# Attention and feed-forward block: kept instruction order in the front, one norm scaling, and the down projection by seven block products

## The chip, the cores and the metric

The kernel runs on one core of one Trainium2 chip. The metric is the device time of one execution in microseconds (us). Times shown are those of three runs; beside them one execution was taken by the hardware profiler. TensorE (PE) multiplies matrices, VectorE (DVE) and ScalarE (ACT) work elementwise, GpSimd (POOL) works elementwise too, and SyncE (SP) issues most transfers.

## The reference, cut to what matters

All values are fp32. There are 8 batches of 128 tokens with 512 features.

```python
n  = layernorm(x)                              # over the features, no weights
r  = n * rsqrt(mean(n*n) + 1e-5) * ln_weight   # a second norm of the same rows
q, k, v = r @ Wq.T, ctx @ Wk.T, ctx @ Wv.T     # 32 heads of 128
p  = softmax(q k^T + bias, masked)             # no scaling by the head size
x1 = x + n + (p v) @ Wo.T
m  = layernorm(x1)
h  = silu((m @ Wg.T) * ag) * ((m @ Wu.T) * au) # 1376 wide
y  = x1 + (h @ Wd.T) * ad
```

## The kernel before, in words

All tokens (1024) are worked on together. The heads come in eight groups of four. Large products are not taken directly: each operand is cut into 2 x 2 blocks, and the product is put together from seven block products instead of eight. Their operands are sums and differences of blocks, called S1, S2, S4 (made by `sums_a`, L215 to L221, of the weights) and T1, T2, T4 (made by `sums_b`, L223 to L229, of the tokens), and one difference that overwrites a block on each side (L219, L227). `seven` (L248) goes through the products in the order 2, 1, 6, 7, 4, 5, 3; ScalarE copies some results out of PSUM (L259, L269), VectorE adds the others to them (L264, L275). Products 6, 7 and 4 go into the banks of product 1, so each waits until the result before it was read.

The stages, in order:

- *Front.* The keys and values of group 0 are made from the context (`kv`, L396), as soon as the weights and the context land. Between their products, `norm1` (L183) makes both norms of each batch of x: moments on VectorE, a square root on ScalarE and a reciprocal on VectorE, y = (x - mean) * rstd on VectorE, a square with accumulation on ScalarE, a second root and reciprocal, and a second scaling on ScalarE. `norm1_T` (L202) transposes the result on PE and writes it into hT with the norm's weight. `combine_tokens` (L239) makes the token sums of the context (ctx_sb) and then of hT. GpSimd makes the weight sums S_k, S_v and S_q.
- *Queries* of all eight groups, written to DRAM (L437 to L446).
- *Attention*, group by group, with the keys and values of the next group between the heads' products.
- *Output projection* with the seven products, the residual (`residual`, L580) and the second norm.
- *Feed-forward.* Eleven slices of 128 of the inner width, the last 96 wide. Slices 2i and 2i+1 are one round of the loop at L724: `seven` again, with gate and up side by side. GpSimd makes the sums S_g and S_u of the weights of the coming round. `gated` (L687) then takes a sigmoid on ScalarE and two multiplications on VectorE; the gatings of a round are called during the next.
- *Down projection* (L762). For each batch, eleven matmuls over the slices collect in one bank (the last batch in two halves). VectorE multiplies by ad (L774) and adds the residual x1 (L775), and SyncE stores the rows (L776).

In what order each engine takes its instructions is set by a scheduler from the program, its costs and its dependencies; program order is one input to it. Where an engine is wrapped in `InOrder` (L37), each call is marked to stay in program order relative to the other marked calls of that engine:

```python
def call(*args, **kw):
    return self.tc.keep_in_program_order(getattr(self.engine, op)(*args, **kw))
```

Before the change only TensorE is wrapped so, and only for the last group of the attention. Tiles with one tag share a fixed number of buffers; a tile waits until the buffer it takes over is free.

Of the kernel before, what the change touches and what calls it, by code (L numbers as in the profile page):

```python
# [10 lines left out]
F32 = mybir.dt.float32  # L11
# [38 lines left out]
def xattn_ffn_kernel(  # L50
# [97 lines left out]

    lnw_sb = const.tile([P, DC], F32, name="lnw_sb")
# [81 lines left out]
    def combine_rows(name, w):  # L231
# [5 lines left out]
        return sums_a(nc.gpsimd, a11, a12, a21, a22, s1, s2, s4)  # L237

    def combine_tokens(src):  # L239
# [6 lines left out]
        return sums_b(nc.vector, b11, b12, b21, b22, t1, t2, t4, nc.gpsimd)  # L246

    def seven(name, tiles, product, part, pool, tag="mm"):  # L248
# [13 lines left out]
        for t in tiles:  # L262
            product(1, t, m[t], True)
            nc.vector.tensor_tensor(part(1, 1, t), part(1, 1, t), m[t], ADD)  # L264
            yield
# [6 lines left out]
        for i, r, c in ((5, 2, 2), (3, 1, 2)):  # L272
            for t in tiles:
                product(i, t, m[t], i == 5)
                nc.vector.tensor_tensor(part(r, c, t), part(r, c, t), m[t], ADD)  # L275
                yield
# [119 lines left out]
    def kv(g, out):  # L396
# [3 lines left out]
        keys = project_T(f"k{g}", combine_rows(f"k{g}", wk), ctx_t, kT)  # L400
# [258 lines left out]
    actp = pool("act", NI, reuse_waits="tile")  # L659
# [160 lines left out]
```

## Time and profile before

| what | value |
|---|---|
| median of 3 runs | 1146.57 us (1145.29 to 1150.09) |
| profiled execution | 1144.65 us |
| its span, first to last instruction | 1142.9 us |
| mean granted TensorE clock | 0.994 |
| first query matmul starts | 68.25 us |
| first down-projection matmul starts | 1063.34 us |
| last store is issued | 1140.1 us |

The profile gives each engine's busy time, the instructions in order of time with what ended the idle time before each, and the chain of work that ended last. Line numbers are those of the kernel before. "PEld" is the loading of weights into TensorE, which overlaps its matmuls. An fp32 matmul leaves two records on PE.

### The profile page before, as it was taken

The page shows a single profiled execution, that of the slowest core. Times are in us where ns is not written, and L with a number is a line of the kernel's source. Part 1 is how long each engine was busy: PE and PEld are TensorE (multiplying, and loading weights), DVE is VectorE, ACT ScalarE, POOL GpSimd, SP SyncE. Part 2 cuts the span into 40 slices and gives each one's busy share as a digit, 9 for nine tenths or more (in the row PEclk, how much of TensorE's full clock was granted, in tenths as well). Part 3 has the DMA queues.
Part 4 walks back from the last instruction along what each step waited for, and adds up shares of the span by engine and source line. Part 5 has one row for each costly group of instructions (what it writes and reads, how often), then busy time and mean ns, then how long its engine had stood idle before and what let it go on. Part 6 is the DMA issues. An engine that isn't in the chain of part 4 may idle for free.

```text
span 1142.9 us, 12312 instructions
## 1 busy us (share of the span) xinstructions
PE 1116.1 (98%) x4286; PEld 729.4 (64%) x4286; DVE 505.2 (44%) x957; ACT 317.5 (28%) x899; POOL 298.4 (26%) x255
## 2 busy tenths in 40 slices
PE   7899999999999999999999999889999999999998
PEld 3564444445867778685868679778888864444445
DVE  4541111116555565555555767653434342434311
ACT  2511112223343444443443443221000022233000
POOL 5531221116333333332311633510000314220000
PEclk9999999999999999999999999989999999999999
DMA  9114433257646555565555466765232602110000
GB/s 281 47 37 146 177 119 111 110 183 263 181 133 208 157 184 167 175 194 168 178 166 165 144 193 217 228 198 159 90 104 63 227 8 74 37 37 1 18 28 28
DMA packets 117533, 154.38 MB, mean 135 GB/s; under 512 B 12032, under 2 KB 71680, under 8 KB 117472
## 3 DMA queue, kind: packets, MB, share of 16 engines
q1 hardware_dynamic: 114784, 149.93, 41.0%
q10 hardware_dynamic: 2192, 2.10, 0.6%
q0 software_dynamic: 496, 1.58, 0.5%
q8 instruction: 34, 0.56, 0.2%
q14 instruction: 27, 0.22, 0.1%
HBM read 101.14 MB, written 52.43 MB: 134 GB/s over the span
## 4 chain that ended last, share of the span: by engine, by line
PE 90%; DVE 4%; DMA 3%; ACT 1%; issue 1%; POOL 0%; SPq 0%; ACTq 0%; DVEq 0%; POOLq 0%
PE mm_q L285 17%; PE mm_v L303 16%; PE mm_k L285 14%; PE m L500 13%; PE mm_f L739 9%; PE dn L770 7%; PE sc L325 4%; PE m L45 4%; PE av L381 4%; DMA a<-att 1%; DMA wv<-in_wvT_dram 1%; ACT s L335 1%; PE av L45 1%; PE tp L176 1%; PE gp L704 1%
## 5 line engine op out<-in xcount | busy, mean ns | idle before, releaser
L320 POOL TENSOR_TENSOR s<-pb,mneg 128x512 f32<-128x512 f32 x64 | 81.6, 1275 | 278.9 <-DVE tt L358 238.6
L285 PE MATMUL mm_k<-ctx_sb,wk 128*128 128x512 f32 x256 | 119.4, 610 | 8.8 <-DMA wk<-in_wkT_dram 4.7
L303 PE MATMUL mm_v<-wv,ctx_sb 128*128 128x256 f32 x512 | 115.9, 379 | 0.5 <-DMA wv<-in_wvT_dram 0.5
L285 PE MATMUL mm_q<-hT,wq 128*128 128x512 f32 x256 | 112.5, 592 | 0.0
L335 ACT ACTIVATE s<-s,nmx 128x128 f32<-128x128 f32 x256 | 99.5, 390 | 34.5 <-DVE nmx L332 34.5
L303 PEld LDWEIGHTS mm_v<-wv,ctx_sb 128*128 128x128 f32 x512 | 95.3, 190 | 14.5 <-DMA wv<-in_wvT_dram 1.3
L386 ACT COPY aT<-av 128x512 f32<-128x512 f32 x64 | 37.5, 585 | 210.9 <-issue 125.4
L285 PE MATMUL mm_k<-ctx_sb,S_k 128*128 128x512 f32 x192 | 87.2, 598 | 3.6 <-POOL S_k L218 2.6
L285 PEld LDWEIGHTS mm_q<-hT,wq 128*128 128x128 f32 x256 | 48.6, 190 | 60.8 <-issue 60.7
L285 PEld LDWEIGHTS mm_k<-ctx_sb,wk 128*128 128x128 f32 x256 | 47.6, 195 | 62.5 <-issue 42.1
L303 PE MATMUL mm_v<-S_v,ctx_sb 128*128 128x256 f32 x384 | 86.7, 381 | 0.0
L285 PE MATMUL mm_q<-hT,S_q 128*128 128x512 f32 x192 | 85.0, 592 | 0.0
L328 DVE TENSOR_TENSOR s<-sc,s 128x512 f32<-128x512 f32 x64 | 44.1, 689 | 85.6 <-PE sc L325 73.8
L303 PEld LDWEIGHTS mm_v<-S_v,ctx_sb 128*128 128x128 f32 x384 | 71.6, 190 | 10.5 <-DVE v L275 1.5
L770 PE MATMUL dn<-wd,act 128*128 128x512 f32 (+3 forms) x198 | 75.8, 545 | 0.0
L275 DVE TENSOR_TENSOR q<-q,mm_q 128x512 f32<-128x512 f32 x32 | 22.0, 687 | 114.9 <-PE mm_q L285 114.9
L500 PE MATMUL m<-wo,a 128*128 128x256 f32 x300 | 72.6, 379 | 0.0
L325 PEld LDWEIGHTS sc<-k,q 128*128 128x128 f32 x448 | 58.7, 192 | 14.8 <-issue 13.4
L285 PEld LDWEIGHTS mm_q<-hT,S_q 128*128 128x128 f32 x192 | 36.5, 190 | 45.9 <-issue 45.9
L285 PEld LDWEIGHTS mm_k<-ctx_sb,S_k 128*128 128x128 f32 x192 | 35.0, 190 | 47.6 <-issue 35.4
L770 PEld LDWEIGHTS dn<-wd,act 128*128 128x128 f32 (+1 forms) x198 | 37.6, 190 | 38.5 <-issue 37.4
L500 PEld LDWEIGHTS m<-wo,a 128*128 128x128 f32 x300 | 56.5, 190 | 7.4
(168 smaller groups left out, 1609.5 us busy)
## 6 DMA issues: line engine op xcount, KB each, us to landing
queries<-q SPq DMA_DIRECT2D x32, 512.0 KB, 3.7
q<-queries SPq DMA_DIRECT2D x32, 512.0 KB, 4.4
turned<-tt SPq DMA_DIRECT2D x64, 256.0 KB, 2.2
pT<-turned SPq DMA_DIRECT2D x256, 64.0 KB, 2.4
att<-aT SPq DMA_DIRECT2D x64, 256.0 KB, 2.3
a<-att SPq DMA_DIRECT2D x32, 512.0 KB, 3.4
wq<-in_wqT_dram SPq DMA_DIRECT2D x8, 1024.0 KB, 5.4
wk<-in_wkT_dram SPq DMA_DIRECT2D x7, 1024.0 KB, 5.8
```

The lines of the kernel that those rows point to most:

```text
L45: return self.tc.keep_in_program_order(getattr(self.engine, op)(*args, **kw))
L285: nc.tensor.matmul(out, w[i][:, c, bass.ts(t, P)], src[i][:, c, :], start=(first and c == 0), stop=(c == HC - 1), skip_group_check=True,)
L303: nc.tensor.matmul(out[:, bass.ts(k, HW)], src[i][:, c, bass.ts(2 * t + k, S)], w[i][:, c, :], start=(first and k == 0 and c == 0), stop=( ...
L320: nc.gpsimd.tensor_tensor(s, pb, mneg[:, b : b + 1, :].to_broadcast([P, GH, S]), ALU.add)
L325: tensor.matmul(sc[:, j, :], qT[:, j, bass.ts(b % 2, S)], kT[j][:, cols], start=True, stop=True)
L328: nc.vector.tensor_tensor(s, sc, s, ALU.add)
L335: nc.scalar.activation(s[:, j, :], s[:, j, :], AF.Exp, bias=nmx[:, j : j + 1], accum_out=sm[:, j : j + 1],)
L381: tensor.matmul(av[:, j, :], v[b // 2][:, b % 2, bass.ts(j, P)], pT[:, :, j, :], start=True, stop=True,)
L386: nc.scalar.copy(aT, av)
L500: tensor.matmul(m[n], sa[n][:, c, :], wo_t[g][n][:, c, :], start=(g == order[0] and c == 0 and k % 2 == 0), stop=(g == order[-1] and c == ...
L739: nc.tensor.matmul(out, ws[t][n][:, c, :], h2_t[n][:, c, :], start=(first and c == 0), stop=(c == HC - 1), skip_group_check=True,)
L770: nc.tensor.matmul(o, act[ic][:m, bass.ts(b, S)], wd[:m, ic, cols], start=(n == 0), stop=(n == NI - 1),)
```

## The change

Four things change.

- *Order.* VectorE and GpSimd are wrapped in `InOrder` from the start up to the queries. The context's sums are called one by one between the key products (`ctx_sums`), the four sums of each weight stay together, and the moments, the scaling and the transposes of a batch are placed at written positions. The wrapped work includes the sums of hT.
- *One norm scaling.* Both norms become one scaling by 1/sqrt(v (1 + eps) + eps^2), with v the variance: no y, no square, no second root; ScalarE scales and shifts x directly. The first norm's own rstd, which the residual needs, is made for all batches at once.
- *Down projection by seven products.* The inner slices in pairs (even, odd), the batches b and b + 4, and the two halves of the output columns are the blocks. `weigh_down` multiplies wd by ad on GpSimd and makes its differences there, one step at each `seven` product of rounds 1 to 3, in kept order. `a_sums` makes the sums of the gated values on VectorE. For each pair of batches `down` takes seven products over five pairs of slices and four matmuls for the last slice; `down_out` adds the results into x1 on ScalarE, VectorE and GpSimd, and x1 is stored.
- *Tiles.* The gated values lie in three tiles instead of eleven, and the sigmoid's tile comes from the work pool.

```diff
@@ -146,6 +146,9 @@
         nc.sync.dma_start(x_in[b // 2][:, b % 2, :], x[b])
     q_w = {0: load_q(0)}
+    vector, gpsimd = InOrder(tc, nc.vector), InOrder(tc, nc.gpsimd)
...
@@ -180,28 +183,30 @@
     mv1 = const.tile([P, B, 2], F32, name="mv1")
     rs1 = const.tile([P, B], F32, name="rs1")
-    def norm1(b):
+    def norm1_moments(b):
         st = small.tile([P, nc.vector.BN_STATS_DIM], F32, tag="st", name=f"st_{b}")
         xb = x_in[b // 2][:, b % 2, :]
-        moments(mv1, b, st, xb)
-        rs = rs1[:, b : b + 1]
-        rstd_of(rs, mv1[:, b, 1:2], 1.0)
-        y = work.tile([P, D], F32, tag="s", name=f"y_{b}", bufs=3)
-        nc.vector.tensor_scalar(
-            y, xb, mv1[:, b, 0:1], rs, ALU.subtract, ALU.mult
-        )
-        sq = work.tile([P, D], F32, tag="aT", name=f"sq_{b}")
-        ss = small.tile([P, 1], F32, tag="ss", name=f"ss_{b}")
-        nc.scalar.activation(sq, y, AF.Square, accum_out=ss)
+        vector.bn_stats(st, xb)
+        vector.bn_aggr(mv1[:, b, :], st)
         rr = small.tile([P, 1], F32, tag="rr", name=f"rr_{b}")
-        rstd_of(rr, ss, 1.0 / D)
+        vector.tensor_scalar(rr, mv1[:, b, 1:2], 1.0 + EPS, EPS * EPS, ALU.mult, ALU.add)
+        nc.scalar.activation(rr, rr, AF.Sqrt)
+        return b, rr
+    def norm1_scale(b, rr):
+        xb = x_in[b // 2][:, b % 2, :]
+        vector.reciprocal(rr, rr)
+        nm = small.tile([P, 1], F32, tag="nm", name=f"nm_{b}")
+        vector.scalar_tensor_tensor(nm, mv1[:, b, 0:1], -1.0, rr, ALU.mult, ALU.mult)
         hn = work.tile([P, D], F32, tag="pT", name=f"hn_{b}", bufs=4)
-        nc.scalar.activation(hn, y, AF.Copy, scale=rr)
+        nc.scalar.activation(hn, xb, AF.Identity, bias=nm, scale=rr)
         return b, hn
     def norm1_T(b, hn):
         tp = transposed(hn, ps_tp.tile([P, DC, P], F32, tag="pt", name="tp"))
-        nc.vector.tensor_tensor(
+        vector.tensor_tensor(
             hT[:, :DC, bass.ts(b, S)], tp, lnw_sb.unsqueeze(2).to_broadcast([P, DC, P]), ALU.mult
         )
@@ -234,16 +239,22 @@
...
-        return sums_a(nc.gpsimd, a11, a12, a21, a22, s1, s2, s4)
-    def combine_tokens(src):
+        return sums_a(gpsimd, a11, a12, a21, a22, s1, s2, s4)
+    def token_sums(src):
...
-        return sums_b(nc.vector, b11, b12, b21, b22, t1, t2, t4, nc.gpsimd)
+        sums = [
+            partial(vector.tensor_tensor, t1, b12, b11, SUB),
+            partial(vector.tensor_tensor, t2, b22, t1, SUB),
+            partial(gpsimd.tensor_tensor, b12, b22, b12, SUB),
+            partial(vector.tensor_tensor, t4, b21, t2, SUB),
+        ]
+        return {1: b11, 2: b21, 3: b22, 4: t4, 5: t1, 6: t2, 7: b12}, sums
     def seven(name, tiles, product, part, pool, tag="mm"):
@@ -397,34 +408,46 @@
...
-        keys = project_T(f"k{g}", combine_rows(f"k{g}", wk), ctx_t, kT)
+        rows_k = combine_rows(f"k{g}", wk)
+        keys = project_T(f"k{g}", rows_k, ctx_t, kT)
         if g:
             yield from keys
             yield from project_V(f"v{g}", combine_rows(f"v{g}", wv), ctx_t, v, ps_mm)
         else:
-            yield from itertools.islice(keys, 4)
+            ctx_sums[0]()
+            yield from itertools.islice(keys, 3)
+            ctx_sums[1]()
+            ctx_sums[2]()
+            yield from itertools.islice(keys, 1)
             values = project_V(f"v{g}", combine_rows(f"v{g}", wv), ctx_t, v, ps, "sc")
             yield from itertools.islice(values, 4)
+            ctx_sums[3]()
             yield from keys
             yield from values
     queries = [dram.tile([P, GH, T], F32, name=f"queries_{g}") for g in range(NG)]
-    ctx_t = combine_tokens(ctx_sb)
+    ctx_t, ctx_sums = token_sums(ctx_sb)
     kvs = {}
-    normed = []
+    normed, transposed1 = [], 0
+    scales = []
     for n, _ in enumerate(kv(0, kvs)):
-        if n % 2 == 1 and 5 <= n < 5 + 2 * B:
-            normed.append(norm1((n - 5) // 2))
-        if n % 2 == 1 and 11 <= n < 11 + 2 * B:
+        if n in (3, 6, 8, 9, 10, 12, 14, 16):
+            scales.append(norm1_moments(len(scales) + len(normed) + transposed1))
+        if n in (6, 8, 9, 10, 12, 14, 16, 18):
+            normed.append(norm1_scale(*scales.pop(0)))
+        if n in (10, 11, 12, 14, 16, 18, 20, 22):
             norm1_T(*normed.pop(0))
-    for n in normed:
-        norm1_T(*n)
-    h_t = combine_tokens(hT)
+            transposed1 += 1
+    h_t, h_sums = token_sums(hT)
+    for form in h_sums:
+        form()
+    vector, gpsimd = nc.vector, nc.gpsimd
     res_scale = const.tile([P, B], F32, name="res_scale")
     res_bias = const.tile([P, B], F32, name="res_bias")
+    rstd_of(rs1, mv1[:, :, 1], 1.0)
...
@@ -678,14 +701,45 @@
...
-    act = [actp.tile([P, T], F32, tag="act", name=f"act_{ic}") for ic in range(NI)]
+    act_even, act_odd = (
+        actp.tile([P, NP, T], F32, tag=f"act{k}", name=f"act_{k}") for k in range(2)
+    )
+    act_rest = actp.tile([P, T], F32, tag="act2", name="act_2")
+    act = [(act_odd if ic % 2 else act_even)[:, ic // 2, :] for ic in range(NI - 1)] + [act_rest]
+    t_tags = [("pb", 2), ("pb", 2), ("tt", 2), ("tt", 2), ("s", 3), ("s", 3), ("s", 3), ("aT", 2)]
+    wd_t = {}
+    def weigh_down(wd):
+        tiles = [
+            work.tile([P, 2, HW], F32, tag=tag, name=f"T_d{k}", bufs=n)
+            for k, (tag, n) in enumerate(t_tags)
+        ]
+        spare = iter([t[:, h] for t in tiles for h in range(2)])
+        for n in range(1, 8):
+            wd_t[n] = []
+        for ic in range(NI):
+            m = min(P, INTER - ic * P)
+            yield partial(gpsimd.tensor_tensor, wd[:m, ic], wd[:m, ic], ad_sb[:m], ALU.mult)
+            if ic % 2:
+                b11, b12 = wd[:, ic - 1, :HW], wd[:, ic - 1, HW:]
+                b21, b22 = wd[:, ic, :HW], wd[:, ic, HW:]
+                t1, t2, t4 = next(spare), next(spare), next(spare)
+                for n, t in enumerate((b11, b21, b22, t4, t1, t2, b12)):
+                    wd_t[n + 1].append(t)
+                yield partial(gpsimd.tensor_tensor, t1, b12, b11, SUB)
+                yield partial(gpsimd.tensor_tensor, t2, b22, t1, SUB)
+                yield partial(gpsimd.tensor_tensor, b12, b22, b12, SUB)
+                yield partial(gpsimd.tensor_tensor, t4, b21, t2, SUB)
...
-    def gated(act, gate, up, ic, m, sg):
+    def gated(act, gate, up, ic, m):
+        sg = work.tile([P, 512], F32, tag="pT", name=f"sg_{ic}", bufs=4)[:m]
...
@@ -705,8 +759,7 @@
...
-        sg = work.tile([P, 512], F32, tag="pT", name=f"sg_{th}", bufs=4)
-        gated(act[ic][:m, bass.ts(th, 512)], o[0][:m], o[1][:m], ic, m, sg[:m])
+        gated(act[ic][:m, bass.ts(th, 512)], o[0][:m], o[1][:m], ic, m)
...
@@ -734,6 +787,9 @@
         if i == 0:
             wd = load_down()
+            gpsimd = InOrder(tc, nc.gpsimd)
+            down_sums = list(weigh_down(wd))
...
@@ -749,31 +805,107 @@
                 last_slice(1)
             if 4 <= n < 12 and n % 2 == 0 and gatings:
                 gatings.pop(0)()
+            if 0 < i < NP - 1 and down_sums:
+                down_sums.pop(0)()
         for r in range(2):
             ic = 2 * i + r
-            sg = acts.tile([P, T], F32, tag="a", name=f"sg_{ic}")
             for cols in (bass.ts(0, 512), bass.ts(1, 512)):
                 gatings.append(partial(
-                    gated, act[ic][:, cols], gate[r][:, cols], act[ic][:, cols], ic, P, sg[:, cols]
+                    gated, act[ic][:, cols], gate[r][:, cols], act[ic][:, cols], ic, P
                 ))
     for gating in gatings:
         gating()
-    for b in range(B):
-        r = work.tile([P, D], F32, tag="aT", name=f"r_{b}")
-        parts = 1 if b + 1 < B else 2
-        for k in range(parts):
-            cols = bass.ts(k, D // parts)
-            o = ps.tile([P, D // parts], F32, tag="m", name=f"dn_{b}_{k}")
-            for n, ic in enumerate([NI - 1, *range(NI - 1)]):
-                m = min(P, INTER - ic * P)
-                nc.tensor.matmul(
-                    o, act[ic][:m, bass.ts(b, S)], wd[:m, ic, cols],
-                    start=(n == 0), stop=(n == NI - 1),
-                )
-            nc.vector.tensor_tensor(r[:, cols], o, ad_sb[:, cols], ALU.mult)
-            nc.vector.tensor_tensor(r[:, cols], r[:, cols], x1[b // 2][:, b % 2, cols], ALU.add)
-            nc.sync.dma_start(out[b][:, cols], r[:, cols])
...
+    def a_sums(b, parts):
+        s = [acts.tile([P, NP, S], F32, tag="a", name=f"S{k}_d{b}") for k in range(3)]
+        up, dn = bass.ts(b, S), bass.ts(b + HB, S)
+        for sl in parts:
+            sums_a(
+                nc.vector, act_even[:, sl, up], act_odd[:, sl, up],
+                act_even[:, sl, dn], act_odd[:, sl, dn], *(t[:, sl, :] for t in s),
+            )
+        return {
+            1: act_even[:, :, up], 2: act_odd[:, :, up], 3: s[2], 4: act_odd[:, :, dn],
+            5: s[0], 6: s[1], 7: act_even[:, :, dn],
+        }
+    LAST = {2: (0, 0), 3: (0, 1), 4: (1, 0), 8: (1, 1)}
+    ORDER = (2, 1, 6, 7, 4, 5, 8, 3)
+    def down(b, sa, last):
+        names = [(2, 1), (6, 7), (4, 5)] + ([(8,), (3,)] if last else [(8, 3)])
+        m = {}
...
+        todo = [(n, i) for n in ORDER for i in range(-1, NP)]
+        if b == 0:
+            todo.sort(key=lambda ni: ni[1])
+        todo = [(n, i) for n, i in todo if (n in LAST if i < 0 else n < 8)]
...
+        for n, i in todo:
+            out, _ = m[n]
+            bank = next(k for k, ns in enumerate(names) if n in ns)
+            if i < 0:
+                r, c = LAST[n]
+                lhs = act_last[:m_last, bass.ts(b + r * HB, S)]
+                rhs = w_last[:m_last, bass.ts(c, HW)]
+            else:
+                lhs, rhs = sa[n][:, i, :], wd_t[n][i]
+            nc.tensor.matmul(
+                out, lhs, rhs, start=bank not in started,
+                stop=(i == NP - 1 or n == 8), skip_group_check=True,
+            )
+            started.add(bank)
+        return {n: o for n, (o, _) in m.items()}, both
+    def down_out(b, m, both, last):
+        r1, r2 = x1[b // 2][:, b % 2, :], x1[(b + HB) // 2][:, b % 2, :]
+        u = work.tile([P, 2, HW], F32, tag="pT", name=f"du_{b}", bufs=4)
+        w = work.tile([P, HW], F32, tag="pT", name=f"dw_{b}", bufs=4)
+        nc.scalar.copy(u[:, 0], m[1])
+        nc.vector.tensor_tensor(r1[:, :HW], r1[:, :HW], m[2], ADD)
+        nc.gpsimd.tensor_tensor(r1[:, :HW], r1[:, :HW], u[:, 0], ADD)
+        nc.vector.tensor_tensor(u[:, 1], u[:, 0], m[6], ADD)
+        nc.vector.tensor_tensor(w, u[:, 1], m[7], ADD)
+        nc.gpsimd.tensor_tensor(r1[:, HW:], r1[:, HW:], u[:, 1], ADD)
+        nc.vector.tensor_tensor(r2, r2, both[:].rearrange("p a n -> p (a n)"), ADD)
+        nc.vector.tensor_tensor(
+            r2.rearrange("p (a n) -> p a n", a=2), r2.rearrange("p (a n) -> p a n", a=2),
+            w.unsqueeze(1).to_broadcast([P, 2, HW]), ADD,
+        )
+        nc.vector.tensor_tensor(r1[:, HW:], r1[:, HW:], m[5], ADD)
+        nc.vector.tensor_tensor(r2[:, HW:], r2[:, HW:], m[8], ADD)
+        nc.sync.dma_start(out[b + HB], r2)
+        if last:
+            nc.sync.dma_start(out[b][:, :HW], r1[:, :HW])
+        nc.vector.tensor_tensor(r1[:, HW:], r1[:, HW:], m[3], ADD)
+        nc.sync.dma_start(*((out[b][:, HW:], r1[:, HW:]) if last else (out[b], r1)))
+    sa = a_sums(0, (slice(0, NP - 1), slice(NP - 1, NP)))
+    for b in range(HB):
+        coming = a_sums(b + 1, (slice(0, NP),)) if b + 1 < HB else None
+        last = b + 1 == HB
+        down_out(b, *down(b, sa, last), last)
+        sa = coming
```

More of the change, by code (lines that the diff above doesn't have):

```diff
@@ L263, in seven @@
             product(1, t, m[t], True)
-            nc.vector.tensor_tensor(part(1, 1, t), part(1, 1, t), m[t], ADD)
+            vector.tensor_tensor(part(1, 1, t), part(1, 1, t), m[t], ADD)
             yield
@@ L274, in seven @@
                 product(i, t, m[t], i == 5)
-                nc.vector.tensor_tensor(part(r, c, t), part(r, c, t), m[t], ADD)
+                vector.tensor_tensor(part(r, c, t), part(r, c, t), m[t], ADD)
                 yield
@@ L658, in xattn_ffn_kernel @@
     wdp = pool("wdp", reuse_waits="tile")
-    actp = pool("act", NI, reuse_waits="tile")
+    actp = pool("act", reuse_waits="tile")
     NP = NI // 2
@@ L760, in xattn_ffn_kernel @@
         gating()
[L762 to L776 removed]
+    HB = B // 2
@@ new lines, in xattn_ffn_kernel @@
+    act_last, w_last = act[NI - 1], wd[:, NI - 1]
+    m_last = INTER - (NI - 1) * P
+    def a_sums(b, parts):
[10 more added lines that the diff above has]
+        }
@@ new lines, in xattn_ffn_kernel @@
+    LAST = {2: (0, 0), 3: (0, 1), 4: (1, 0), 8: (1, 1)}
[3 more added lines that the diff above has]
+        m = {}
+        for k, ns in enumerate(names):
+            t = (
+                ps.pools[1].tile([P, 2, HW], F32, tag="tp", name=f"d{k}_{b}", bufs=1)
+                if k == 3 and b % 2 else ps.tile([P, 2, HW], F32, tag="m", name=f"d{k}_{b}")
+            )
+            for h, n in enumerate((5, 4) if ns == (4, 5) else ns):
+                m[n] = t[:, 1 - h if ns == (4, 5) else h, :], n == ns[0]
+            if ns == (4, 5):
+                both = t
+        todo = [(n, i) for n in ORDER for i in range(-1, NP)]
+        if b == 0:
+            todo.sort(key=lambda ni: ni[1])
+        todo = [(n, i) for n, i in todo if (n in LAST if i < 0 else n < 8)]
+        first_of = {}
+        for n, i in todo:
+            first_of.setdefault(n, i)
+        started = set()
+        for n, i in todo:
+            out, _ = m[n]
[12 more added lines that the diff above has]
+        return {n: o for n, (o, _) in m.items()}, both
@@ new lines, in down_out @@
+    def down_out(b, m, both, last):
[12 more added lines that the diff above has]
+            w.unsqueeze(1).to_broadcast([P, 2, HW]), ADD,
+        )
+        nc.vector.tensor_tensor(r1[:, HW:], r1[:, HW:], m[5], ADD)
[5 more added lines that the diff above has]
+        nc.sync.dma_start(*((out[b][:, HW:], r1[:, HW:]) if last else (out[b], r1)))
```

## The prediction

> **What bounds the kernel now.** I read the page first: its span, its engines' busy shares and the chain that ended last.
>
> ```profile
> span 1142.9 us, 12312 instructions
> PE 1116.1 (98%) x4286; PEld 729.4 (64%) x4286; DVE 505.2 (44%) x957; ACT 317.5 (28%) x899; POOL 298.4 (26%) x255
> PE 90%; DVE 4%; DMA 3%; ACT 1%; issue 1%; POOL 0%; SPq 0%; ACTq 0%; DVEq 0%; POOLq 0%
> ```
>
> TensorE (PE) is busy 98% of the span and makes 90% of the chain. A gain comes either from fewer matmuls or from one of the few places where PE stands still. So next I listed the waits of PE over the whole span (few: the largest single ones are 4.7 us for the first load, 4.5 us for a load of attention results, 3.4 us and 2.6 us early on) and then cut the start into stretches. The columns are length, busy us (and count) of PE, weight loads, VectorE, ScalarE, GpSimd, then granted clock, DMA share, GB/s.
>
> ```profile
> 16.00:21.40 5.40, 5.40 (x21) 3.61 (x19) 4.79 (x10) 0.75 (x2) 4.86 (x3) 1.00 1.05 385
> 21.40:28.60 7.20, 4.08 (x9) 1.35 (x8) 7.20 (x22) 3.37 (x11) 7.20 (x6) 1.00 0.93 197
> 28.60:32.00 3.40, 0.03 (x1) 0.07 (x1) 3.34 (x13) 3.03 (x11) 3.40 (x3) 1.00 0.25 73
> 32.00:35.00 3.00, 3.00 (x5) 1.18 (x6) 2.40 (x12) 2.45 (x7) 2.92 (x4) 0.61 0.00 0
> 35.00:38.00 3.00, 3.00 (x10) 1.49 (x9) 1.98 (x11) 2.30 (x10) 1.21 (x1) 0.83 0.01 3
> ```
>
> PE is full to 21.4 us, nearly idle to 32 and then runs at a clock of 0.61 and 0.83. The timelines of PE, GpSimd (POOL) and VectorE (DVE) say what was late:
>
> ```profile
> 24.13 1.98 PE L285 MATMUL mm_k<-ctx_sb,S_k 128*128 128x512 f32 x4 [2.62 <-POOL S_k L218]
> 26.55 1.98 PE L285 MATMUL mm_k<-ctx_sb,S_k 128*128 128x512 f32 x4 [0.44 <-DVE rr L166]
> 31.97 5.37 PE L285 MATMUL mm_k<-ctx_sb,wk 128*128 128x512 f32 x8 [3.43 <-ACT k L269]
> ...
> 17.25 2.31 POOL L217 TENSOR_TENSOR S_v<-wv 128x512 f32<-128x512 f32 x1 [0.55 <-DMA wv<-in_wvT_dram]
> 19.52 3.33 POOL L227 TENSOR_TENSOR ctx_sb<-ctx_sb 128x1024 f32<-128x1024 f32 x1
> 22.82 1.26 POOL L218 TENSOR_TENSOR S_k<-S_k,wk 128x512 f32<-128x512 f32 x1
> ...
> 22.78 0.67 DVE L264 TENSOR_TENSOR k<-k,mm_k 128x512 f32<-128x512 f32 x1
> 25.85 0.65 DVE L264 TENSOR_TENSOR k<-k,mm_k 128x512 f32<-128x512 f32 x1
> ```
>
> S_k, which key product 6 needs, sits behind two longer GpSimd sums. The two additions that free product 6's banks (ready when product 1 ends, about 16.3 and 18.1) wait behind norm work on VectorE to 22.8 and 25.9. ScalarE's copy after product 6 sits behind squares and norms, and PE waits for it.
>
> Last, the down projection, by form, and the chain's rate for 128x256 matmuls:
>
> ```profile
> L770 PE MATMUL dn<-wd,act 128*128 128x512 f32 x140 | 61.2, 592 | 0.0
> 49.39 3.46 PE mm_v L303 x16
> 1063.34 75.78 PE L770 MATMUL dn<-wd,act 96*128 96x512 f32 x198
> ```
>
> It idles nowhere: only fewer matmul columns can shorten it. A matmul has two records, so 8 matmuls of 256 columns take 3.46 us, 0.4325 each.
>
> **What the Trainium skill says.** "TensorE: Matmul & The Clock Gate", What's actually happening: after an idle window of about 3.4 us the clock falls to half until PE has been busy about as long. The trace agrees: no slowing after the 2.62 us gap, 0.61 after the one of 3.43 us. "PSUM — Partial Sum Buffer", Engine vs sequencer instructions: the queues of VectorE, ScalarE and GpSimd are strict FIFO, which is what delays the two additions above. "SBUF — State Buffer", Who interferes with whom: a VectorE instruction with two SBUF inputs contends with GpSimd. The trace agrees: the same 128x1024 subtraction on hT took 1.22 us beside an idle GpSimd and 3.00 us beside a busy one.
>
> **The change, part by part.**
>
> *Front (order kept, one norm scaling).* From 21.4 to the first query matmul at 68.25 PE takes 46.85 us. The work is ten halves: five key products of two tiles (3.44 us each in the chain), five value products (3.46), eight transposes (0.44): 17.2 + 17.3 + 3.5 = 38.0. Lost: 8.85 us (idle about 7.1, slow clock about 1.7). The new order, walked with the durations above:
> - GpSimd: the four S_k sums follow each other from 15.0 (1.69, then 1.45 each: to 21.1), then the 1024-wide context difference (3.33: 24.4), then S_v. Product 6 needs the second sum (about 18.2), product 7 the difference at 21.4 + 3.44 = 24.8.
> - VectorE: t1 to 15.6, first key addition to 17.0, t2 to 18.2, second addition to 18.9: product 6 can start at 21.4. Then moments of x0, value additions at 19.8 and 21.6, t4 at 22.2 (1.2 to 1.7), moments of x1 to x3 (0.67 plus three small instructions each).
> - ScalarE loses eight squares (0.62) and their accumulator reads, and gets the scaling directly from x (0.72). The first copy after product 6 is ready at 23.1, the second at 24.8; ahead of the second stands the scaling of x1, which waits for the moments of x1 and the VectorE work before them, about 25.2. So the copy ends about 25.8; its product 7 tile starts after 24.8 + 1.72 + 0.44 = 27.0. Later transposes and copies have 1.5 us or more.
>
> So PE should run through to 59.4. The SyncE queue is unchanged in order; the query weight loads are released by PE's last reads and move along with it. One wait is new. On GpSimd the hT difference now stands behind all four sums of the third query weights, which start only when the last value matmul is done (59.4). Contended these take 2.25 + 2.13 + 1.26 + 1.26 as their like did at 69.6, the difference 2.35 to 3.3: done at 68.7 to 69.7. Query product 7 wants it at 59.4 + 3 x 3.44 = 69.7. Behind it on GpSimd stand only sums for later query groups. VectorE's hT sums now come after all value additions (60.1) and end near 66 even if one is contended; product 6 needs the second at 66.3. I charge 0.5 us for both margins (none to 2): **-8.4 us**. From there to the feed-forward the order on PE, and nearly all others, is as before; the waits there follow PE and shift with it.
>
> *Feed-forward.* GpSimd gains 11 scalings of wd (128x512, 1.26 as S_q: 13.9 us) and 20 differences (128x256, 0.72 as S_g: 14.4 us). It idles 8.75, 18.39 and 18.39 us between slices' sums and wholly after 1019; wd was issued at 902.9 and 910.9 and landed within 12.5 us. Ahead of the sums of slice 2 come 13.4 us (six scalings, eight differences): 955.3 + 13.4 + 6.2 = 975 against PE's need near 997. The cost is contention: VectorE's two gating instructions took 2.13 us beside GpSimd, 1.41 alone. Rounds are spaced 24.59 us three times and 24.03 once, the difference being a wait for a VectorE addition. The new order puts five gating instructions ahead of it, but starts them earlier: alone it ends 1.2 us before its need, contended up to 1 us after. From -1.7 to +2; I take **0**.
>
> *Down projection.* Before: 88 matmuls' worth of 512 columns, 75.78 us. After: for each of four pairs of blocks seven products over five slices and four for the last slice: 39 matmuls of 256 columns, 156 x 0.4325 = 67.5 us. Weight loads rise from 198 to 312, but take 190 ns against 216 ns of streaming, as in mm_v. **-8.3 us**. The sums it needs are on VectorE: those of slices 0 to 3 for the first pair run inside the last round; the last slice's gating ends near 1068.3 (old clock) and its five small sums by 1070; PE needs them after 4 + 28 matmuls, at 1063.3 + 13.8 = 1077. The twelve 640-wide sums (0.82 each, from 0.69 for 512) end near 1079.5, ahead of the first output's additions. Those free banks for the third pair, needed at 1097; they take about 4 us. Without that cover the exposed piece would be the 9.8 us of sums.
>
> *Tail.* Last addition once instead of twice (-0.4), but a 256 KB store is issued just ahead of the last 128 KB (+0 to +0.4; stores landed in 2.0 and 1.7 us): **-0.2**.
>
> Sum: -8.4 + 0 - 8.3 - 0.2 = -16.9: span 1126.0, with the 1.75 us around it 1127.7. The median of the runs shown stands 1.9 above that profiled execution, giving 1129.7. I take 1129.0.
>
> **Rivals.**
> 1. *The front's gain goes* (0.15): VectorE now waits in order; if a moment or a transpose is late, all behind it is, and an idle window of 3.4 us with its slow clock comes back later. For it: margins of 0.5 to 1.2 us at product 7. Against it: each slip is under 2 us by the durations shown. Only the down gain stays: 1137 to 1138.
> 2. *The down gain goes* (0.06): PE waits for the last slice's sums or for banks. Slack is 7 and 12 us. Then 1137.
> 3. *Slower* (0.05): GpSimd's 28.3 us of weight sums delay the sums of the next gate and up slices, and PE waits every round. It decides only once the 13.4 us ahead of slice 2 take over 35 us; to end slower by 0.5% they need about 58 us, over four times their rows. Then 1152 or more.
> 4. *No effect* (0.04): a wait outside the trace's PE order holds the chain, so that both gains end in it. The attention's waits follow PE; only a load not released by PE could do it.
>
> The likeliest case (0.70) has its own range 1126 to 1132. The range to hold 8 in 10 takes in rivals 1 and 2 in most part: 1125 to 1138. Half a per cent (5.7 us) is about what a measurement can tell here: faster 0.91, same 0.04, slower 0.05.
>
> **What would show it.** Right: key product 6 starts at 21.4, no granted clock under 0.9 between 21 and 60, first query matmul near 59.4, 312 down-projection records over 67.5 us, GpSimd busy some 34 us more (28.3 and eight additions of 0.72), rounds still about 24 to 25 us. Wrong: a PE wait over 2 us for a ScalarE key copy, the hT difference on GpSimd, or VectorE's S_d sums; or rounds beyond 26 us.

## The result, and the profile after

The changed kernel takes 1133.88 us (median of 4 runs, 1133.11 to 1134.89) against 1146.05 for the kernel before on the same chip (4 runs, among them the three shown before: 1145.29 to 1150.09). The ratio is 0.9887, interval 0.9863 to 0.9912: faster by 1.1%. The forecast was 1129.0 with a range of 1125 to 1138. Sign and range held; the gain was 12.2 us where 16.9 were forecast, and the likeliest case's own range (1126 to 1132) was missed by 1.9 us.

The profiled execution took 1133.11 us. These are lines of its page, as shown of the kernel before: the span, the busy shares and the chain by engine.

```profile
span 1131.3 us, 12597 instructions
PE 1105.0 (98%) x4400; PEld 749.2 (66%) x4400; DVE 527.6 (47%) x977; ACT 315.4 (28%) x880; POOL 340.1 (30%) x294
PE 88%; DVE 6%; DMA 3%; ACT 1%; issue 1%; POOL 0%; SPq 0%; ACTq 0%; DVEq 0%; POOLq 0%
```

PE's busy time, which includes what a slow clock adds to it, fell by 11.1 us, nearly the whole change of the span (-11.6). But VectorE's share of the chain rose from 4% to 6%: PE now waits for it in places where it did not before. GpSimd is busy 41.7 us longer (298.4 to 340.1; forecast 34).

The stretches of the start, with the same columns as in the prediction:

```profile
21.40:28.60 7.20, 6.21 (x19) 2.95 (x18) 6.99 (x13) 1.89 (x5) 7.12 (x5) 1.00 0.81 187
28.60:32.00 3.40, 2.26 (x9) 1.25 (x9) 2.71 (x11) 3.16 (x7) 3.32 (x3) 1.00 0.24 70
32.00:35.00 3.00, 3.00 (x12) 1.54 (x11) 2.70 (x7) 1.61 (x5) 3.00 (x4) 1.00 0.00 0
```

From 28.6 to 32 us PE was almost idle before; now it works 2.26 of 3.40 us, and the clock of 0.61 at 32 us is gone. What is left is a hole around 29 us. The timelines of PE, ScalarE, VectorE and GpSimd show what made it:

```profile
29.74 1.98 PE L296 MATMUL mm_k<-ctx_sb,wk 128*128 128x512 f32 x4 [2.13 <-ACT k L280]
...
28.40 0.81 ACT L204 ACTIVATE hn<-x,nm,rr 128x512 f32<-128x512 f32 x1 [1.16 <-DVE nm L45]
29.12 0.56 ACT L280 COPY k<-mm_k 128x512 f32<-128x512 f32 x1
...
22.35 1.35 DVE L45 SCALAR_TENSOR_TENSOR nm<-mv,rr 128x1 f32<-128x1 f32 x1
27.11 1.26 DVE L45 SCALAR_TENSOR_TENSOR nm<-mv,rr 128x1 f32<-128x1 f32 x1
...
21.33 2.34 POOL L45 TENSOR_TENSOR ctx_sb<-ctx_sb 128x1024 f32<-128x1024 f32 x1
27.09 1.26 POOL L45 TENSOR_TENSOR wv<-wv 128x512 f32<-128x512 f32 x1
```

Read from the top: PE waits for a copy of key results on ScalarE; the copy stands behind the scaling of batch 1 of x (`hn`; called "the scaling of x1" from here on, as in the prediction, though the residual has that name too); the scaling waited for its shift `nm` on VectorE. `nm` is one number per partition. Two of these took 1.35 and 1.26 us, and they end (23.70 and 28.37) when the GpSimd instruction beside them ends (23.67 and 28.35). A later one of 0.63 us ends so too (at 34.63, GpSimd's instruction at 34.61); with none running one takes 0.16 us.

A second, smaller wait stands at the queries: the query additions are behind three hT sums on VectorE.

```profile
63.01 6.21 DVE L45 TENSOR_TENSOR hT<-hT 128x1024 f32<-128x1024 f32 x3
69.14 1.27 DVE L275 TENSOR_TENSOR q<-q,mm_q 128x512 f32<-128x512 f32 x2
69.96 2.38 PE L296 MATMUL mm_q<-hT,S_q 128*128 128x512 f32 x5 [0.72 <-DVE q L275]
```

In the feed-forward the timelines of PE and VectorE in the first full round after round 0 show waits where the kernel before had at most 0.3 us:

```profile
967.92 1.96 PE L795 MATMUL mm_f<-T_h,S_g 128*128 128x512 f32 x4 [1.50 <-DVE gate L275]
970.54 1.96 PE L795 MATMUL mm_f<-T_h,S_u 128*128 128x512 f32 x4 [0.67 <-DVE act L275]
...
962.03 2.88 DVE L747 SCALAR_TENSOR_TENSOR act<-act,au_sb,sg 128x512 f32<-128x512 f32 x2
964.84 1.21 DVE L744 SCALAR_TENSOR_TENSOR sg<-gate,ag_sb,sg 128x512 f32<-128x512 f32 x1
966.08 1.09 DVE L747 SCALAR_TENSOR_TENSOR act<-act,au_sb,sg 128x512 f32<-128x512 f32 x1
967.10 0.67 DVE L275 TENSOR_TENSOR gate<-gate,mm_f 128x512 f32<-128x512 f32 x1
```

The addition at 967.10 frees the bank that PE wants. It stands behind gatings which take 1.1 to 1.4 us each; in the kernel before two took 1.41 together when GpSimd was idle.

The down projection, in the chain and by form, and the last work on VectorE and SyncE:

```profile
1060.45 67.39 PE d L873 x312
...
L873 PE MATMUL d<-wd,act 128*128 128x256 f32 x120 | 28.5, 379 | 0.0
...
1127.87 0.42 DVE L900 TENSOR_TENSOR x<-x,d 128x256 f32<-128x256 f32 x1 [0.88 <-PE d L873]
1128.32 0.33 SPq L901 DMA_DIRECT2D out_dram<-x  x1
```

312 records in 67.39 us where 198 took 75.78, with no wait in front of any of them. (The chain enters this stage at 1060.45; by the timeline its first matmul starts at 1060.29, so the stage takes 67.55 us.)

Where the span's 11.6 us come from, by the start of each stage (before, after):

| point | before | after | gain so far |
|---|---|---|---|
| first query matmul | 68.25 | 62.20 | 6.05 |
| first gate addition of round 0 (product 1) | 942.72 | 936.55 | 6.17 |
| first down-projection matmul | 1063.34 | 1060.29 | 3.05 |
| end of the span | 1142.9 | 1131.3 | 11.6 |

Between the queries and the feed-forward the 0.72 us lost at the query wait was more than made up: the stretch from 700 to 800 us has a mean granted clock of 0.95 before and 0.97 after, following waits of 4.5 and 5.1 us for a load of attention results. Of the three variants below whose edits lie in the feed-forward alone, two had 0.95 and one 0.98, so it varies without a change ahead of it. So I put this 0.8 us down to the execution profiled, not to the change; that is argued, not shown.

### The profile page after: what moved, and what is told of

The parts are those of the page before. It is cut to its first block, busy times and chain, and to the rows that moved or that the text cites. A ratio compares the mean times of both kernels' runs of the same rounds, so it can differ in the third digit from the quotient of the medians.

```text
span 1131.3 us, 12597 instructions
## 1 busy us (share of the span) xinstructions
PE 1105.0 (98%) x4400; PEld 749.2 (66%) x4400; DVE 527.6 (47%) x977; ACT 315.4 (28%) x880; POOL 340.1 (30%) x294
## 4 chain that ended last, share of the span: by engine, by line
PE 88%; DVE 6%; DMA 3%; ACT 1%; issue 1%; POOL 0%; SPq 0%; ACTq 0%; DVEq 0%; POOLq 0%
PE mm_q L296 16%; PE mm_v L314 16%; PE mm_k L296 14%; PE m L523 13%; PE mm_f L795 8%; PE d L873 6%; PE sc L336 4%; PE av L392 4%; PE m L45 4%; DVE sg L744 1%; DMA wk<-in_wkT_dram 1%; ACT s L346 1%; DMA a<-att 1%; DVE act L747 1%; PE av L45 1%
## 5 line engine op out<-in xcount | busy, mean ns | idle before, releaser
L314 PEld LDWEIGHTS mm_v<-S_v,ctx_sb 128*128 128x128 f32 x384 | 71.8, 190 | 11.1 <-DVE v L286 1.5
L336 PE MATMUL sc<-k,q 128*128 128x128 f32 x448 | 58.9, 275 | 0.0
L392 PE MATMUL av<-pT,v 128*128 128x128 f32 x424 | 56.0, 275 | 0.0
```

Of the source, the lines that this page charges most:

```text
L314: nc.tensor.matmul(out[:, bass.ts(k, HW)], src[i][:, c, bass.ts(2 * t + k, S)], w[i][:, c, :], start=(first and k == 0 and c == 0), stop=( ...
L336: tensor.matmul(sc[:, j, :], qT[:, j, bass.ts(b % 2, S)], kT[j][:, cols], start=True, stop=True)
L392: tensor.matmul(av[:, j, :], v[b // 2][:, b % 2, bass.ts(j, P)], pT[:, :, j, :], start=True, stop=True,)
```

## The experiments

All ratios are to the kernel before, run on the same chip beside the variant. Intervals are given where a run was repeated.

**Each part alone.** The front alone is the kernel before with the diff's first hunks (order and norm scaling, first below), the down part alone with the others (second below).

```diff
+    vector, gpsimd = InOrder(tc, nc.vector), InOrder(tc, nc.gpsimd)
...
+    for form in h_sums:
+        form()
```

```diff
+            down_sums = list(weigh_down(wd))
...
+            down_out(b, *down(b, sa, last), last)
```

> The kernel before with the front part of the change alone (kept order, one norm scaling). Theory: the front gives what the changed kernel's profile shows, a first query matmul near 62.2 us against 68.25, less 0.7 us of a wait at query product 6: about 1140.5 us, the feed-forward rounds as before (24.6, 24.6, 24.6, 24.0 us) and the down projection 75.8 us. Rival: the front alone gives the 8.4 us that were forecast and loses part of it to the down part: 1137.7 us.

> The kernel before with the down part alone (seven products, sums of wd in kept order on GpSimd, new tiles for the gated values). Theory: 67.5 us for the down projection, but rounds 1 to 3 of the feed-forward longer by 3 us in sum than before, as in the changed kernel: about 1140.6 us; first query matmul at 68.3. Rival: the longer rounds come from the two parts together, and this part alone gives its full 8.5 us: 1137.6 us.

Measured: front alone 1139.56 us, ratio 0.9945 (0.9927 to 0.9963); down part alone 1139.8, ratio 0.9944 (0.9927 to 0.9962). The front alone has its first query matmul at 61.98 and both front waits, and rounds of 24.6, 24.6, 24.6 and 24.0 us. The down part alone has the front of the kernel before (68.38) and the long rounds (26.6, 25.3, 24.9). Waits of PE from 955 to 1070 us, first of the front alone, then of the down part alone (us in total, times, longest):

```profile
PE mm_f L762 <- DVE gate L275: 1.0, 3, 0.3
```

```profile
PE mm_f L772 <- DVE gate L264: 1.8, 3, 1.4
PE mm_f L772 <- DVE act L264: 1.4, 3, 0.7
```

So the two parts add up within what the intervals tell, 6.3 and 6.4 us by their ratios, and neither is seen to take from the other. The longer rounds belong to the down part.

**What the kept order is worth.** Three variants leave the norm's new form and places, but take the marks of program order off both engines, off GpSimd, or off VectorE: one of the three added lines each, in this order.

```diff
-    vector, gpsimd = InOrder(tc, nc.vector), InOrder(tc, nc.gpsimd)
+    vector, gpsimd = nc.vector, nc.gpsimd
+    vector, gpsimd = InOrder(tc, nc.vector), nc.gpsimd
+    vector, gpsimd = nc.vector, InOrder(tc, nc.gpsimd)
```

> The changed kernel with VectorE and GpSimd not wrapped in the front: the scheduler orders them freely, the one norm scaling and the written places of the norm's calls stay. The key additions then stand behind the moments of five batches again, and the first sum of S_v ahead of the second of S_k. Theory (the kept order is what brings most of the front's 6 us): PE waits over 2 us for the key additions or ScalarE's copies, first query matmul at 65 us or later against 62.2, time 1137 or more against 1133.9. Rival (less norm work is what brings it): first query matmul at 62.5 or earlier, time 1134.5 or less.

> The changed kernel with only VectorE kept in program order in the front, GpSimd free; of the instructions up to the queries only the first sum of S_v moves, to ahead of the last three of S_k. Theory (VectorE's order carries the front's gain, since GpSimd's first S_v sum delays S_k and the context difference by 1.3 to 2.3 us and TensorE needs them later than that): first query matmul at 61.5 to 63 us, time 1133 to 1135. Rival (both orders are needed): product 6 or 7 waits over 2 us for GpSimd, first query matmul at 65 or later, time 1137 or more.

> The changed kernel with only GpSimd kept in program order in the front, VectorE free: the key additions stand behind the moments of several batches. Theory (VectorE's order carries the gain): as with both free, first query matmul at 70 us or later against 62.2, time 1140 to 1145. Rival (GpSimd's order carries it): first query matmul at 64 or earlier, time 1136 or less.

Measured: both free 1144.5 us, ratio 0.9978 (0.9967 to 0.999), first query matmul 73.40; only VectorE kept 1133.18, ratio 0.9904 (0.9874 to 0.9934), 62.73; only GpSimd kept 1145.37 (a little over the range expected), ratio 0.9995 (0.9983 to 1.0008), 76.61. Waits of PE between 15 and 80 us, first with only VectorE kept, then with only GpSimd kept:

```profile
PE mm_k L296 <- ACT k L280: 2.3, 1, 2.3
PE mm_q L296 <- DVE q L275: 0.7, 1, 0.7
```

```profile
PE mm_k L296 <- ACT k L280: 4.9, 1, 4.9
PE mm_v L314 <- ACT v L270: 3.0, 1, 3.0
PE mm_v L314 <- DVE v L286: 2.1, 1, 2.1
PE mm_k L296 <- DVE rr L200: 0.7, 1, 0.7
PE mm_k L296 <- DVE k L275: 0.6, 1, 0.6
```

VectorE's order carries the front's gain. Keeping GpSimd's as well brought nothing that can be told from nothing, although S_v ahead of S_k looked like the first cause of delay in the profile of the kernel before. And the lighter norm alone is no gain: with VectorE free, the first query matmul comes 5 to 8 us later than before the change. What the lighter norm adds where the order is kept is not known: no variant keeps the order with both norms. After the wait of 4.9 us the clock falls to 0.50, as the Trainium skill says of idle windows of about 3.4 us ("TensorE: Matmul & The Clock Gate", What's actually happening); after the 2.13 us of the changed kernel it stays at 1.00.

**The shift of the norm.** `nm` takes two tensors from SBUF, the mean and rr. The first edit gives rr as a per-partition scalar, so that one tensor is left. The second leaves `nm` alone and cuts GpSimd's 1024-wide difference beside it into four.

```diff
-        vector.scalar_tensor_tensor(nm, mv1[:, b, 0:1], -1.0, rr, ALU.mult, ALU.mult)
+        vector.tensor_scalar(nm, mv1[:, b, 0:1], rr, -1.0, ALU.mult, ALU.mult)
```

```diff
-            partial(gpsimd.tensor_tensor, b12, b22, b12, SUB),
+            lambda: [
+                gpsimd.tensor_tensor(b12[:, c, k], b22[:, c, k], b12[:, c, k], SUB)
+                for c in range(HC) for k in (slice(0, 256), slice(256, 512))
+            ],
```

> The changed kernel with the 128x1 shift of the norm made by an instruction with one tensor input (the scale as a per-partition scalar) in place of one with two tensor inputs. Theory: the two shifts that took 1.35 and 1.26 us waited for GpSimd's instruction in progress; now each takes about 0.15 us, the second key copy on ScalarE comes 2.3 us earlier, the 2.1 us wait of key product 7 goes, first query matmul near 60.1: about 1131.8 us. Rival: what is late there is VectorE's queue as such (moments and t4 ahead of the shift), and the wait stays at 1.5 us or more: 1133 to 1134 us.

> The changed kernel with GpSimd's context difference (and hT difference) as four instructions of 128x256 in place of one of 128x1024; the shift nm keeps its two tensor operands. Theory (such a VectorE instruction stands until the GpSimd instruction in progress ends, however small it is itself): the shift of x0, which falls beside this difference, takes 0.2 to 0.8 us in place of 1.35, ending with one of the four pieces; the shift of x1, beside a 128x512 sum of S_v, still ends with that sum. Rival (it is slowed by sharing the memory, or is slow for its own form): 1.2 to 1.4 us again.

VectorE's timeline with one tensor operand:

```profile
22.10 0.21 DVE L45 TENSOR_SCALAR nm<-mv,rr 128x1 f32<-128x1 f32 x1
25.64 0.21 DVE L45 TENSOR_SCALAR nm<-mv,rr 128x1 f32<-128x1 f32 x1
```

The timelines of VectorE and GpSimd with two tensor operands and the difference cut in four (the second line of GpSimd is the last two of the four pieces alone):

```profile
21.96 0.41 DVE L45 SCALAR_TENSOR_TENSOR nm<-mv,rr 128x1 f32<-128x1 f32 x1
25.25 0.72 DVE L45 SCALAR_TENSOR_TENSOR nm<-mv,rr 128x1 f32<-128x1 f32 x1
...
20.95 3.77 POOL L45 TENSOR_TENSOR ctx_sb<-ctx_sb 128x256 f32<-128x256 f32 x4
22.32 2.40 POOL L45 TENSOR_TENSOR ctx_sb<-ctx_sb 128x256 f32<-128x256 f32 x2
24.69 1.26 POOL L45 TENSOR_TENSOR S_v<-wv 128x512 f32<-128x512 f32 x1
```

With one tensor operand both shifts take 0.21 us, the wait for the key copy falls to 0.2 us, and the first query matmul comes at 59.69, 2.5 us sooner: 1131.89 us, ratio 0.9871 (0.9852 to 0.9891), an interval that overlaps that of the changed kernel. (The profiled execution was only 0.7 us shorter: at the first gate addition of round 0, 935.17 against 936.55, 1.1 of the 2.5 us were gone, and from there to the down projection it took 0.9 us more.) With the difference in pieces the shift of x0 takes 0.41 us and ends at 22.37, just after the third piece has begun (22.32), and that of x1, now beside a sum that ends at 25.95, ends at 25.97; PE's wait for the copy is 0.54 us and the first query matmul starts at 60.14. This variant was run once, at 1132.95. So the shift is not slow in itself, nor merely slowed by sharing: it stands until GpSimd's instruction is over. The Trainium skill ("SBUF — State Buffer", Who interferes with whom) says that two-input VectorE instructions contend with GpSimd and that the shared port pair is an exclusive lock; it also says ("DVE: scalar operands, raw-bit mode, write accounting and state across instructions", Scalar operands) that a per-partition scalar does not take up the second tensor stream. Both agree with these runs, the first down to an instruction of one element per partition.

**The feed-forward.** First, the weight sums of the down projection are left out: neither the scaling by ad nor the differences of wd are made, and the seven products read wd as it is (their number stays).

```diff
-            yield partial(gpsimd.tensor_tensor, wd[:m, ic], wd[:m, ic], ad_sb[:m], ALU.mult)
...
-            if 0 < i < NP - 1 and down_sums:
-                down_sums.pop(0)()
```

> The changed kernel without the scaling of wd by ad and without the differences of wd on GpSimd (left out; the seven products take unscaled blocks in their place, as many matmuls as before). Theory: GpSimd's work slows VectorE's gating in rounds 1 to 3; without it the round from the second to the third takes 24.6 us or less, not 26.7, and the time is near 1131.5 us, some of the rest staying because the sums of the next weights contend too. Rival: it is the new order of the gating on VectorE (a gating instruction that waits for its sigmoid ahead of the addition that PE needs); then the rounds stay at 26.7, 25.3 and 24.9 us and the time at 1133.9 us.

Then nothing is left out, but VectorE is kept in program order from the weight sums on (in both gating instructions and in the additions of `seven`), so that a round's gatings come after the two additions of product 1 that PE waits for (first diff); and last, the weight sums are also called later in a round (both diffs).

```diff
-        nc.vector.scalar_tensor_tensor(
+        vector.scalar_tensor_tensor(
...
-            gpsimd = InOrder(tc, nc.gpsimd)
+            vector, gpsimd = InOrder(tc, nc.vector), InOrder(tc, nc.gpsimd)
```

```diff
-            if 0 < i < NP - 1 and down_sums:
+            for _ in range(1 + (n > 11) if 0 < i < NP - 1 and n > 3 and down_sums else 0):
                 down_sums.pop(0)()
```

> The changed kernel with VectorE kept in program order in the feed-forward too, so that the gatings of a round come after the two additions of product 1 that TensorE waits for, and outside most of GpSimd's S_g and S_u sums. GpSimd's sums of wd stay as they are. Theory (an addition that PE needs stands behind gatings that GpSimd makes long): no wait for an addition over 0.4 us, rounds of 24.6 and 24.0, the 3 us are back: time near 1131, span near 1128.3. Rival (GpSimd's sums of wd make S_g late, or the additions themselves long): rounds stay at 25 to 26.7 and the time at 1133 to 1134.

> As the run before, and the steps of wd's sums are called only after the fourth step of a round, two at each of its last two steps, so that they fall behind S_g, S_u and less beside the gatings. Theory: nothing more is to be had, since the additions no longer wait: within 0.5 us of the run before, near 1131. Rival (the sums of wd still delay S_g or S_u at the start of a round): a further gain of 0.5 to 1.5 us.

The table gives the time from the first gate addition of round 0 to the first down-projection matmul, by the timelines; a round without any wait takes 24.03 us.

| kernel | this stretch | of it, over the shortest | median, ratio |
|---|---|---|---|
| before | 120.62 | 1.66 | |
| changed | 123.74 | 4.78 | 1133.88, 0.9887 |
| no sums of wd | 122.17 | 3.21 | 1132.26, 0.9876 (0.9859 to 0.9893) |
| gatings in kept order | 120.34 | 1.38 | 1131.48, 0.9861 (0.9847 to 0.9876) |
| and later sums of wd | 118.96 | 0 | 1130.09, 0.9846 (0.9829 to 0.9864) |

With all of GpSimd's new work gone, half of what was lost to the kernel before was back (1.6 of 3.1 us), and no more: the rounds took 24.9, 24.9 and 25.5 us, which is neither the theory's 24.6 nor the rival's 26.7, 25.3 and 24.9. With the order mended and all of that work still there, everything was back in the trace. VectorE's timeline of the last variant shows how:

```profile
967.06 0.69 DVE L45 TENSOR_TENSOR gate<-gate,mm_f 128x512 f32<-128x512 f32 x1 [4.53 <-PE mm_f L795]
968.77 0.69 DVE L45 TENSOR_TENSOR act<-act,mm_f 128x512 f32<-128x512 f32 x1 [1.03 <-PE mm_f L795]
969.38 1.47 DVE L45 SCALAR_TENSOR_TENSOR sg<-gate,ag_sb,sg 128x512 f32<-128x512 f32 x1
970.88 1.10 DVE L45 SCALAR_TENSOR_TENSOR act<-act,au_sb,sg 128x512 f32<-128x512 f32 x1
```

The additions now wait for PE (4.53 and 1.03 us idle before them) and not PE for them. The gatings behind them still take 1.1 to 1.6 us beside GpSimd, but nothing waits for them. My theory that later sums would bring nothing more does not fit the traces: with the gatings in order alone, one wait was left,

```profile
983.26 1.96 PE L795 MATMUL mm_f<-h,S_u 128*128 128x512 f32 x4 [1.14 <-DVE act L45]
```

for an addition of product 5 behind a contended gating (980.88, 1.64 us). The last variant has no wait there at all. The gain of 1.4 us is in this stretch of one execution each; the last variant's profiled execution reached it 2.0 us later and was 0.7 us longer as a whole, and the intervals of the two variants' ratios overlap.

**All repairs together**: the shift as one tensor, the third hT sum after the first query additions, the gatings in order, the later sums.

```diff
-    for form in h_sums:
+    for form in h_sums[:3]:
         form()
...
-        for _ in project_T(f"q{g}", combine_rows(f"q{g}", q_w.pop(g)), h_t, heads):
-            pass
+        for n, _ in enumerate(project_T(f"q{g}", combine_rows(f"q{g}", q_w.pop(g)), h_t, heads)):
+            if g == 0 and n == 3:
+                h_sums[3]()
```

> Four repairs together: the shift nm as one tensor operand with a scale, the third hT sum after the first query additions, the gatings in kept order, and the later wd sums. Theory (the parts add up): first query matmul near 59.7, no wait of 0.72 at query product 6, rounds of 24.6, time 1133.9 less 2.5, 0.7 and 3: near 1127.7. Rival (the loads of attention results, which follow the PE only in part, take some of it back): 1129 to 1131.

Measured: 1126.2 us (1125.51 to 1126.76), ratio 0.9818 (0.9803 to 0.9832): faster than both kernels, by 1.8% and, by the two ratios, by some 0.7%. First query matmul 59.47, the rounds as in the last row of the table. Of its waits of PE over 1 us, the first load apart, none is left in the front or the feed-forward. The longest, over the whole span:

```profile
PE m L45 <- DMA a<-att: 8.2, 2, 5.0
PE mm_k L296 <- DMA wk<-in_wkT_dram: 4.4, 1, 4.4
PE m L45 <- DVE S_a L223: 1.9, 1, 1.9
```

It is 1.5 us below the 1127.7 that the sum of the parts gave. That sum counted nothing for the later sums of wd, which in the traces were worth 1.4 us; that this is the difference is likely, not shown. In the middle some 0.8 us of the front's further gain did not arrive: the first gate addition of round 0 comes at 933.88, 2.67 us sooner than in the changed kernel, where the queries gave 3.45.

## Why the prediction was right or wrong

- *Front*: forecast -8.4 to the end of the query waits, measured -6.05 at the first query matmul and +0.72 behind it: -5.3. The mechanism was right: product 6 started at 21.86 (21.4 forecast; the first value load landed 0.5 us later), there was no slow clock, VectorE's order did it. Of the order kept on GpSimd, which the prediction had named first, no gain could be told. The step that failed is "three small instructions each" on VectorE. It counted the 128x1 shifts as small, though the prediction itself named the contention of two-input VectorE instructions with GpSimd, and applied it only to the large ones. So the scaling of x1 began at 28.40 instead of 25.2, and the copy ended at 29.7 instead of 25.8. The run with one tensor operand puts the first query matmul at 59.69, 0.3 us from the forecast 59.4. (The prediction split the 8.85 us lost before into 7.1 idle and 1.7 of slow clock; by the trace PE was busy 40.37 of the 46.85 us, so it was 6.5 and 2.4. The sum is not touched.)
- *The wait at the queries*: charged with 0.5 us at query product 7 for GpSimd's hT difference. That difference was in time (it ended at 72.65, and no wait for it shows). The wait of 0.72 us came at product 6, from query additions queued behind the third hT sum. I had asked when VectorE's sums end, and not which additions stand behind them; the queues are strictly first in, first out, as the prediction had quoted.
- *Feed-forward*: forecast 0 (-1.7 to +2), measured +3.1, outside its bounds. This is the term that was furthest off. That gatings would run ahead of an addition and be contended was seen, but priced for one addition with gatings of 2.13 us a pair. Nearly all of them fell beside GpSimd, two at 2.88 us, and a second addition (`act`) was late too, behind a gating that waited for its sigmoid. The -1.7 us was there as well, as the repaired order shows, but the change's own order did not reach it.
- *Down projection*: -8.3 forecast, -8.2 measured from the first matmul on (-8.4 in the chain), 67.4 us for 312 records; sums and banks were in time. *Tail*: -0.2 and -0.2.
- *Rivals*: the first came true in part; over a third of the front's gain went, 2.13 of the 3.1 us by the very wait named (for a ScalarE key copy), without the slow clock. The second and fourth did not occur; the parts alone gave 6.3 and 6.4 us. The third is false: nothing waited for S_g or S_u. GpSimd's sums cost time by contention with VectorE, not by being late. Two of the stated signs of error were seen: the wait over 2 us for a key copy, and a round beyond 26 us (26.68), this one with all of the down projection's gain still in place.

Together: 3.1 us short in the front, 3.1 in the feed-forward, some 0.8 us given by the middle: 11.6 in place of 16.9. That the time lies in the stated range is in part luck: the range had been made wide for rivals 1 and 2, not for a loss in the feed-forward, and the 0.8 us in the middle were not foreseen.

## What to carry to other kernels

Where a queue is kept in order by hand, list for each consumer what stands ahead of it in that queue, and put the instruction that frees a bank for TensorE first; here VectorE's order decided whether the front gained 6 us or lost 5 to 8 by the first query matmul (both kept: ratio 0.9887; VectorE free and GpSimd kept: 0.9995). Price every VectorE instruction with two SBUF tensors by the GpSimd instruction that may be running beside it, not by its own size, and give a per-partition factor as a scalar operand where that is possible, and look in the trace whether it helped (the last section has one-tensor instructions that waited all the same). New work on an idle engine is free only where the instructions that it slows have slack: here the rounds grew by 3.1 us, half of it from the sums of wd, and by nothing once no addition stood behind the slowed gatings.

## What the runs showed of the hardware that was not expected

A VectorE instruction of one element per partition took 1.35 and 1.26 us instead of 0.16, because a GpSimd instruction of 2.34 or 1.26 us was running; with GpSimd's work cut in four the first took 0.41 us, and with one tensor operand 0.21. The lock works in the other direction too: the same 128x512 sum on GpSimd took 1.26 us alone and up to 2.26 beside VectorE's 1024-wide sums.

One tensor operand alone is not what sets an instruction free. In the changed kernel a scaling of 128x8 with one tensor ends at 46.52, 0.02 us after the GpSimd instruction beside it:

```profile
45.34 1.18 DVE L453 TENSOR_SCALAR res_bias<-res_bias 128x8 f32<-128x8 f32 x1
45.22 1.28 POOL L223 TENSOR_TENSOR S_q<-S_q,wq 128x512 f32<-128x512 f32 x1
```

So does a 128x4 one in the attention (`nmx`, 1.23 us, to 702.26; GpSimd to 702.23), which takes 0.17 us elsewhere. The 128x1 shift with one tensor did not wait. What sets them apart was not tested.
